# Moving the maxima's transfers to the front of a group's first slot, and splitting the shift around the small maximum

## The chip, the cores and the metric

The kernel runs on one NeuronCore of a Trainium2 chip. The metric is device time in microseconds of one execution, given as the median of several runs. The engines are named as the profile names them: PE is TensorE (PEld its weight loads), DVE is VectorE, ACT is ScalarE, POOL is GpSimd, and SP is SyncE, which issues most of the transfers.

## The reference

One transformer block over x of shape (4, 1024, 512) in float32, conditioned on a vector of 128 values per batch entry, with a further residual around the whole block:

```python
def _tc_rmsnorm(x, t, gw, gb, bw, bb):
    g = (t @ gw.T + gb)[:, None, :]
    b = (t @ bw.T + bb)[:, None, :]
    inv_rms = jax.lax.rsqrt(jnp.mean(x * x, axis=-1, keepdims=True) + EPS)
    return g * x * inv_rms + b

def _attention(x, Wq, Wk, Wv, Wo):            # 16 heads of 32
    q, k, v = ((x @ W.T).reshape(B, L, H, dh) for W in (Wq, Wk, Wv))
    p = jax.nn.softmax(jnp.einsum('blhd,bmhd->bhlm', q, k) / scale, axis=-1)
    return jnp.einsum('bhlm,bmhd->blhd', p, v).reshape(B, L, D) @ Wo.T

def _swiglu(x, gate_w, hid_w, out_w):         # hidden width 2048
    return jax.nn.silu(x @ gate_w.T) * (x @ hid_w.T) @ out_w.T

y = x + _attention(_tc_rmsnorm(x, t, g1w, g1b, b1w, b1b), Wq, Wk, Wv, Wo)
y = y + _swiglu(_tc_rmsnorm(y, t, g2w, g2b, b2w, b2b), gate_w, hid_w, out_w)
return x + y
```

## The kernel before

Tokens are handled in 8 blocks of 512 and heads in 4 groups of 4. Attention goes over 64 groups j: one block, one group of heads, and one half of the block's queries (256). A group has four slots (UN = 4), one for each 256 keys, and there are 256 slots r in all. A loop over g issues the work by hand, engine by engine, in program order; `kind = g % 4` is the slot's place in its group. What is done for one slot r is spread over later turns of the loop:

- `scores(r)` at g = r: sixteen TensorE matmuls into the PSUM tile `sc`. There is one such tile of four banks. `keep(r)` has ScalarE copy it to `raw[r]`, and `running_max` folds it into `rmax`.
- After the last slot of a group, at kind 0 of the next group, `max_blocks` transposes `rmax` in 32 by 32 blocks and reduces it on VectorE. `max_T` turns the small result with a matmul, reduces it once more on VectorE (`top`, 32 by 32) and sends it to DRAM (`tops`). `spread` reads it back as 1,024 values for all 128 partitions into the one buffer `shift`. So there are two transfers from SP, of which the second waits for the first to land.
- `shifted(r)` subtracts the maximum at g = r + 5, so that the last slot of a group is shifted at the next group's kind 0 and the next group's first slot at kind 1. `exponential(r)` follows in the same turn.
- `weighted(r)` at g = r + 6 multiplies with the values (`av`), and `accumulate(r)` has GpSimd issue a transfer that adds 1 MB of `raw` to the group's first slot, for the sums of the softmax. There are three of them per group, each waiting for the one before it.
- `take_sums` forms the sums of an earlier group with sixteen matmuls into the spare of the scores' PSUM tile (`spare`), and ScalarE copies them out (`total`). `max_T` uses the same spare tile and is issued after `take_sums`.

`spare` can only be written when `keep` has copied the scores, because it is the same PSUM memory.

What fills the rest of a turn depends on its time. Before g = 60 (about the first 650 us) `chain` issues one projection of keys, queries, values or outputs, and an even turn issues a second one, `late`. After that come the feed-forward products in pairs of turns: an even turn has `pair_26`, `copy_156` and the output products `one()` and `two()`; an odd turn has `pair_7`, `pair_3`, `pair_15`, and at its end `pair_4`, which waits for VectorE's `sub_5`.

TensorE, VectorE, ScalarE and GpSimd run their instructions in the order in which the loop issues them. SP's transfers are put in order by the framework's scheduler, which follows the order of issue and readiness; a transfer on SP that waits holds up those behind it. `pinned` holds the loads of keys, queries and values that belong to a turn.

In an even turn before the change, the order around the edit at kind 0 is, early: `max_blocks`, `shifted`, `late`, pinned loads, `weighted`, `keep`, `exponential`, `chain`, `take_sums`, `max_T`, `spread`, `running_max`. Late: the same up to `keep`, then `load_f`, `pair_26`, `copy_156`, `take_sums`, `max_T`, `exponential`, `one`, `two`, `running_max`, `spread`.

Of the kernel before, what the change touches and what calls it, by code (L numbers as in the profile page):

```python
# [12 lines left out]
ALU = mybir.AluOpType  # L13
# [10 lines left out]
def tile_cond_transformer_block(  # L24
# [13 lines left out]
    nc = tc.nc  # L38
# [8 lines left out]
    HG = P // DH  # L47
# [3 lines left out]
    UN = KT // 2  # L51
# [46 lines left out]
    raw, rmax, shift, av, acc, avs, oT = {}, {}, {}, {}, {}, {}, {}  # L98
# [230 lines left out]
    def spare(g: int):  # L329

        return ps_sc.tile([P, HG, 2, HQ], F32, tag="sc", name=f"spare{g}")

    def max_T(j: int, banks):
        pt = banks[:CHUNKS, 1, 0, :P]
        nc.tensor.matmul(pt, state.pop(("blocks", j)), ident, start=True, stop=True)
        top = sb.tile([CHUNKS, 32], F32, tag="top", name=f"top{j}")
        nc.vector.tensor_reduce(top, pt.rearrange("b (a q) -> b q a", a=P // 32), AX.X, ALU.max)
        state["top", j] = tc.dram_tile([CHUNKS, 32], F32, name=f"tops{j}")
        nc.sync.dma_start(out=state["top", j], in_=top)

    def spread(j: int):

        shift[j] = sb.tile([P, HG, HQ], F32, tag="shift", name=f"shift{j}")
        src = state.pop(("top", j)).rearrange("(o b) q -> o (b q)", o=1)
        nc.sync.dma_start(
            out=shift[j].rearrange("p h q -> p (h q)"), in_=src.to_broadcast([P, HG * HQ])
        )

    def shifted(r: int):
        s = shift[r // UN].unsqueeze(1).to_broadcast(list(raw[r].shape))  # L350
        nc.vector.tensor_tensor(raw[r], raw[r], s, ALU.subtract)  # L351

    def exponential(r: int):
        nc.scalar.activation(raw[r], raw[r], AF.Exp)  # L354
# [43 lines left out]
    def sums_out(j: int):  # L398
        state["total", j] = sb.tile([P, HQ], F32, tag="total", name=f"total{j}", bufs=2)
        nc.scalar.copy(state["total", j], state.pop(("sum", j)))  # L400
# [67 lines left out]
    def tokens(n: int):  # L468
        return [x2[n][:, k : k + 2, i * HQ : (i + 1) * HQ] for k in (0, 2) for i in range(2)]
# [23 lines left out]
    def product(dst, w, moving, start: bool = False):  # L493
        for k in range(2):
            mm(dst, w[:, k, :], moving[:, k, :], start and k == 0, k == 1, True)
# [17 lines left out]
    def pair_26(p: int):  # L513
        a = bank_a[p]
        product(a[:, LEFT], fw[p, 0][:, 1], tokens(p // NF)[2])
        product(a[:, RIGHT], fw[p, 1][:, 1], state["sums"][:, 1])

    def copy_156(p: int):
        if "b" not in state:

            state["b"] = ps_b.tile([P, NB], F32, tag="wb", name="pb")
            nc.tensor.matmul(state["b"], ones_mean, x2[0][:, 0, :], start=True, stop=True)
        bank_b[p] = state["b"]
        nc.scalar.copy(bank_b[p][:, RIGHT], bank_a[p][:, RIGHT])  # L524
# [46 lines left out]
    pinned = {}  # L571
# [36 lines left out]
    for b in range(1, B):  # L608
        for half in range(QB):
            s = math.ceil((len(queue) + 1) / PACE)  # L610
# [72 lines left out]
    with tc.manual_schedule(  # L683
# [37 lines left out]
        g = 0  # L721
# [22 lines left out]
        def take_sums(j: int, banks):  # L744

            if 0 <= j < NR // UN:
                sums(j, banks)
                sums_out(j)
                if j >= direct:
                    inverse(j)  # L750
                    normalize(j)

        while g < END:
            kind = g % UN
            r_x, r_v = g - UN - 1, g - UN - 2
            x_on, v_on = 0 <= r_x < NR, 0 <= r_v < NR
            j_m = g // UN - 1
            m_on = 0 <= j_m < NR // UN
            j_s = g // UN - 2
            s_on = 0 <= j_s < NR // UN  # L760
            j_n = g // UN - 3
            n_on = 0 <= j_n < NR // UN
            ffn = g >= FS
            p = (g - FS) // 2
            even = g % 2 == 0
            columns[0] = DH

            if g < NR:
                scores(g)
            if kind == 0 and m_on:  # L770
                max_blocks(j_m)
            if kind == 1 and j_n == GB + 1:
                normalize(GB)
            if x_on:
                shifted(r_x)
            if late is not None:
                late()
                late = None
            for fn, a in pinned.pop(g, []):
                fn(*a)  # L780
            if v_on:
                weighted(r_v)
                accumulate(r_v)
            if g < NR:
                keep(g)
            if kind == 1 and s_on:
                take_av(j_s)
            if kind == 0 and (m_on or n_on):
                banks = spare(g)
            due = bool(first) and first[0][0] <= g  # L790
            if not ffn:
                if x_on:
                    exponential(r_x)
                evict = chain(g, FG)
                if kind == 0 and n_on:
                    take_sums(j_n, banks)
                if kind == 0 and m_on:
                    max_T(j_m, banks)
                    spread(j_m)
                if g < NR:  # L800
                    running_max(g, 0)
                    running_max(g, 1)
                if evict is not None:
                    evict()
                for fn, a in halfway.pop(g, []):
                    fn(*a)
                if g == FS - 1:
                    columns[0] = DH
                    pair_15(0)
                    take_5(0)  # L810
                    add_15(0)
                elif even:
                    late = chain(g, FG)
                if g in (FS - 4, FS - 2):
                    load_f((g - FS + 4) // 2)
            elif even:
                load_f(p + 2)
                pair_26(p)
                copy_156(p)
                if kind == 0 and n_on:  # L820
                    take_sums(j_n, banks)
                if kind == 0 and m_on:
                    max_T(j_m, banks)
                if x_on:
                    exponential(r_x)
                one, two, evict = filler(p)
                one()
                two()
                if g < NR:
                    running_max(g, 0)  # L830
                    running_max(g, 1)
                if evict is not None:
                    evict()
                if kind == 0 and m_on:
                    spread(j_m)
                for fn, a in halfway.pop(g, []):
                    fn(*a)
            else:
                extra = due or len(queue) > FG
                evict = None  # L840
                if kind == 3 and extra:
                    evict = chain(g)
                pair_7(p)
                sub_5(p)
                pair_3(p)
                if kind == 3:
                    gate_tanh(p)
                if x_on:
                    exponential(r_x)
                pair_15(p + 1)  # L850
                take_5(p + 1)
                for fn, a in amid.pop(g, []):
                    fn(*a)
                if kind == 1:
                    gate_tanh(p)
                    if extra:
                        spare_bank[0] = True
                        evict = chain(g)
                if g < NR:
                    running_max(g, 0)  # L860
                if kind == 3 and evict is not None:
                    evict()
                if kind == 3:
                    gate(p)
                if g < NR:
                    running_max(g, 1)
                add_15(p + 1)
                if kind == 1:
                    gate(p)
                    if evict is not None:  # L870
                        evict()
                pair_4(p)
                hidden(p)
                if due:
                    chain(g)()
                for fn, a in halfway.pop(g, []):
                    fn(*a)
            if kind == 0 and n_on and j_n < direct:
                inverse(j_n)
                if j_n % GB == GB - 1:  # L880
                    normalize(j_n)
            if kind == 2 and n_on and j_n < direct and j_n % GB != GB - 1:

                if j_n != GB:
                    normalize(j_n)
            columns[0] = DH
            for fn, a in ended.pop(g, []):
                fn(*a)
            if g == FS + 2 * FG - 2:
                load_ow(0)  # L890
            g += 1
# [90 lines left out]
```

## Time and profile before

| | |
|---|---|
| median of 3 runs | 2914.73 us (2912.62 to 2918.55) |
| profiled execution | 2911.5 us, span 2909.7 us |
| PE busy | 2449.3 us (84%) |
| DVE busy | 1908.1 us (66%) |
| ACT busy | 1330.1 us (46%) |
| mean granted TensorE clock | 0.924 |
| accumulates (POOL queue) | 192 of 1 MB, 9.3 us to landing (median) |
| broadcasts of the maxima (SP queue) | 64 of 512 KB, 5.1 us to landing (median) |

A line of the profile's groups gives source line, engine, operation, output and inputs, shapes and count; then busy time and mean duration; then how long the engine stood idle just before these instructions and what released it. Names such as `raw` or `pb` are the kernel's tiles with numbers left out. Line 93 is the helper through which most matmuls go, so that its groups are told apart by their tiles. `SPq` and `POOLq` lines are instructions that issue a transfer. In a timeline, the bracket at the end of a line holds the idle time before it and its releaser.

### The profile page before, as it was taken

The page shows a single profiled execution, that of the slowest core. Times are in us where ns is not written, and L with a number is a line of the kernel's source. Part 1 is how long each engine was busy: PE and PEld are TensorE (multiplying, and loading weights), DVE is VectorE, ACT ScalarE, POOL GpSimd, SP SyncE. Part 2 cuts the span into 40 slices and gives each one's busy share as a digit, 9 for nine tenths or more (in the row PEclk, how much of TensorE's full clock was granted, in tenths as well). Part 3 has the DMA queues.
Part 4 walks back from the last instruction along what each step waited for, and adds up shares of the span by engine and source line. Part 5 has one row for each costly group of instructions (what it writes and reads, how often), then busy time and mean ns, then how long its engine had stood idle before and what let it go on. Part 6 is the DMA issues. An engine that isn't in the chain of part 4 may idle for free. (4 is left out here: it accounts for less than half of the span.)

```text
span 2909.7 us, 71319 instructions
## 1 busy us (share of the span) xinstructions
PE 2449.3 (84%) x31866; PEld 1157.2 (40%) x31866; DVE 1908.1 (66%) x2048; ACT 1330.1 (46%) x1303; POOL 172.4 (6%) x205
## 2 busy tenths in 40 slices
PE   8778778888788888887988878887888788889999
PEld 3233223334344443443444434444344344444444
DVE  2667666757667776776677757776678667863332
ACT  4555555555345544554455435544455445532111
POOL 0000000000000000000000000000000000000000
PEclk9899889999899989998999989999999899999999
DMA  5697788877777777777767767777677777773442
GB/s 197 195 242 205 204 218 202 209 176 187 184 187 192 194 188 171 192 185 203 183 178 186 194 174 192 190 196 182 167 197 197 187 184 173 183 206 111 138 134 81
DMA packets 198270, 535.53 MB, mean 184 GB/s; under 512 B 25415, under 2 KB 82759, under 8 KB 170574
## 3 DMA queue, kind: packets, MB, share of 16 engines
q0 software_dynamic: 28656, 208.68, 37.2%
q1 hardware_dynamic: 169022, 322.29, 33.5%
q8 instruction: 251, 4.11, 0.6%
q14 instruction: 53, 0.43, 0.0%
q10 hardware_dynamic: 288, 0.01, 0.0%
HBM read 279.99 MB, written 42.23 MB: 111 GB/s over the span
## 5 line engine op out<-in xcount | busy, mean ns | idle before, releaser
L351 DVE TENSOR_TENSOR raw<-raw,shift 128x2048 f32<-128x2048 f32 x256 | 584.9, 2285 | 418.4 <-DMA shift<-tops 418.4
L354 ACT ACTIVATE raw<-raw 128x2048 f32<-128x2048 f32 x256 | 489.4, 1912 | 600.4 <-DVE raw L351 599.6
L304 ACT COPY raw<-sc 128x2048 f32<-128x2048 f32 x256 | 477.8, 1867 | 364.5 <-PE sc L297 233.4
L309 DVE TENSOR_TENSOR rmax<-rmax,raw 128x1024 f32<-128x1024 f32 x384 | 468.7, 1221 | 40.8 <-ACT raw L304 34.7
L93 PE MATMUL pc<-h,ow 128*32 128x512 f32 x4096 | 477.1, 594 | 0.5 <-DMA ow<-in_out_w 0.5
L93 PE MATMUL pb<-sums,fa 128*32 128x256 f32 x2048 | 170.0, 459 | 271.4 <-DVE pb L531 271.4
L364 PE MATMUL av<-raw,v 128*32 128x256 f32 x4096 | 304.6, 420 | 101.6 <-ACT raw L354 101.4
L297 PE MATMUL sc<-q,k 32*128 32x256 f32 x4096 | 330.5, 442 | 0.1
L378 POOL DMA_DIRECT2D raw<-raw x192 | 165.7, 863 | 2412.1 <-ACT raw L354 1472.1
L297 PEld LDWEIGHTS sc<-q,k 32*128 32x128 f32 x4096 | 206.1, 206 | 205.6 <-issue 127.1
L93 PE MATMUL pa<-x,fa 128*32 128x256 f32 x4096 | 270.0, 381 | 9.9 <-issue 9.2
L93 PE MATMUL pa<-sums,fw 128*32 128x256 f32 x4096 | 268.2, 379 | 0.4 <-issue 0.4
L93 PE MATMUL pkq<-y,wkq 128*32 128x512 f32 (+1 forms) x1976 | 248.0, 623 | 4.1 <-ACT y L183 4.1
L93 PEld LDWEIGHTS pc<-h,ow 128*32 128x32 f32 x4096 | 165.3, 110 | 208.7 <-issue 137.5
L562 DVE SCALAR_TENSOR_TENSOR res<-pc,res 128x512 f32<-128x512 f32 x128 | 88.5, 692 | 196.5 <-PE pc L93 196.5
L364 PEld LDWEIGHTS av<-raw,v 128*32 128x32 f32 x4096 | 113.9, 117 | 255.3 <-ACT raw L354 110.4
L93 PEld LDWEIGHTS pb<-sums,fa 128*32 128x32 f32 x2048 | 69.0, 124 | 346.4 <-DVE pb L531 300.7
L93 PEld LDWEIGHTS pa<-x,fa 128*32 128x32 f32 x4096 | 134.1, 112 | 118.2 <-issue 30.2
L93 PEld LDWEIGHTS pa<-sums,fw 128*32 128x32 f32 x4096 | 132.9, 110 | 89.0 <-issue 0.9
L541 ACT ACTIVATE t<-pa 128x512 f32<-128x512 f32 x128 | 76.7, 599 | 153.6 <-PE pa L93 153.6
L93 PE MATMUL po<-oT,wo 128*32 128x512 f32 x1024 | 127.8, 643 | 14.8 <-DVE h L546 11.7
L524 ACT COPY pb<-pa 128x256 f32<-128x256 f32 x128 | 45.7, 357 | 203.1 <-PE pa L93 182.5
(92 smaller groups left out, 2017.3 us busy)
## 6 DMA issues: line engine op xcount, KB each, us to landing
raw<-raw POOLq DMA_DIRECT2D x192, 1024.0 KB, 9.3
fw<-sw SPq DMA_DIRECT2D x128, 512.0 KB, 7.4
fa<-in_gh_w SPq DMA_DIRECT2D x128, 384.0 KB, 4.3
shift<-tops SPq DMA_DIRECT2D x64, 512.0 KB, 5.1
ow<-in_out_w SPq DMA_DIRECT2D x128, 256.0 KB, 6.2
wkq<-in_kq_w SPq DMA_DIRECT2D x32, 512.0 KB, 6.4
v<-vs SPq DMA_DIRECT2D x128, 128.0 KB, 5.9
k<-kqs SPq DMA_DIRECT2D x124, 128.0 KB, 7.3
```

Of the source, the lines that this page charges most:

```text
L93: nc.tensor.matmul(dst[k : k + n, :], w[:, k : k + n], moving, start=start, stop=stop, skip_group_check=seeded)
L297: nc.tensor.matmul(sc[:, i, k, :], keys[rows, k * P : (k + 1) * P], queries[rows, :], start=True, stop=True)
L304: nc.scalar.copy(raw[r].rearrange("p k h q -> p h k q"), state.pop(("sc", r)))
L309: nc.vector.tensor_tensor(rmax[j], rmax[j], raw[r][:, k, :, :], ALU.max)
L351: nc.vector.tensor_tensor(raw[r], raw[r], s, ALU.subtract)
L354: nc.scalar.activation(raw[r], raw[r], AF.Exp)
L364: nc.tensor.matmul(av[j][i * DH : (i + 1) * DH, :], v[m, u][:, k, i * DH : (i + 1) * DH], raw[r][:, k, i, :], start=(kt == 0), stop=(kt == ...
L378: nc.gpsimd.dma_start(out=acc[j].rearrange("p k h q -> p (k h q)"), in_=raw[r].rearrange("p k h q -> p (k h q)"), accum_op=ALU.add,)
L524: nc.scalar.copy(bank_b[p][:, RIGHT], bank_a[p][:, RIGHT])
L541: nc.scalar.activation(state["t", p], bank_a[p], AF.Tanh, scale=0.5)
L562: nc.vector.scalar_tensor_tensor(r, pp, 0.5, r, ALU.mult, ALU.add)
```

## The change

At kind 0 alone, the shift of the previous group's last slot is cut in two halves of two heads each. The small maximum's matmul, reduction and both transfers are issued between them. `take_sums`, `max_T` and `spread` move ahead of the projection in the early turns, ahead of `load_f` in the late ones, and ahead of the pinned loads in both. The exponential and the pinned loads follow the second half. In late turns `pair_26` and `copy_156` are issued first, as they were, and `load_f` after them. Turns of kind 1 to 3 keep their order.

```diff
-    def shifted(r: int):
-        s = shift[r // UN].unsqueeze(1).to_broadcast(list(raw[r].shape))
-        nc.vector.tensor_tensor(raw[r], raw[r], s, ALU.subtract)
+    def shifted(r: int, heads: slice = slice(0, HG)):
+        t = raw[r][:, :, heads, :]
+        s = shift[r // UN][:, heads, :]
+        nc.vector.tensor_tensor(t, t, s.unsqueeze(1).to_broadcast(list(t.shape)), ALU.subtract)
...
-            if x_on:
+            if x_on and kind:
                 shifted(r_x)
...
-            for fn, a in pinned.pop(g, []):
-                fn(*a)
+            if kind:
+                for fn, a in pinned.pop(g, []):
+                    fn(*a)
...
-            if kind == 0 and (m_on or n_on):
-                banks = spare(g)
+            if kind == 0 and ffn:
+                pair_26(p)
+                copy_156(p)
+            if kind == 0:
+                if m_on or n_on:
+                    banks = spare(g)
+                if n_on:
+                    take_sums(j_n, banks)
+                if x_on:
+                    shifted(r_x, slice(0, HG // 2))
+                if m_on:
+                    max_T(j_m, banks)
+                    spread(j_m)
+                if x_on:
+                    shifted(r_x, slice(HG // 2, HG))
+                for fn, a in pinned.pop(g, []):
+                    fn(*a)
...
                 evict = chain(g, FG)
-                if kind == 0 and n_on:
-                    take_sums(j_n, banks)
-                if kind == 0 and m_on:
-                    max_T(j_m, banks)
-                    spread(j_m)
...
                 load_f(p + 2)
-                pair_26(p)
-                copy_156(p)
-                if kind == 0 and n_on:
-                    take_sums(j_n, banks)
-                if kind == 0 and m_on:
-                    max_T(j_m, banks)
+                if kind:
+                    pair_26(p)
+                    copy_156(p)
...
-                if kind == 0 and m_on:
-                    spread(j_m)
```

## The prediction

> **What bounds the kernel now.** I read the page first, then the waits split at 650 us (before it TensorE projects keys, queries and values between attention slots; after it the feed-forward products are interleaved), then the timeline of one group of four slots in each part. Part five of the page (line, engine, operation, tiles, count, then busy us, mean ns, then idle before it and its releaser):
>
> ```profile
> L351 DVE TENSOR_TENSOR raw<-raw,shift 128x2048 f32<-128x2048 f32 x256 | 584.9, 2285 | 418.4 <-DMA shift<-tops 418.4
> L93 PE MATMUL pb<-sums,fa 128*32 128x256 f32 x2048 | 170.0, 459 | 271.4 <-DVE pb L531 271.4
> L364 PE MATMUL av<-raw,v 128*32 128x256 f32 x4096 | 304.6, 420 | 101.6 <-ACT raw L354 101.4
> ```
>
> TensorE is busy 2449.3 of 2909.7 us; of its 460 us idle, 271 and 101 end on VectorE's sub_5 and on the exponential. Both are queued behind the first shift of a group, which waits for the broadcast of the maxima: 418.4 us over 64 groups. The waits by part say where (us, times, longest). 20 to 650 us:
>
> ```profile
> DVE raw L351 <- DMA shift<-tops: 118.4, 14, 14.9
> PE av L364 <- ACT raw L354: 101.4, 15, 11.1
> DVE top L337 <- PE spare L335: 37.6, 14, 3.4
> PE spare L335 <- ACT total L400: 18.9, 12, 3.4
> ```
>
> 650 to 2600 us:
>
> ```profile
> DVE raw L351 <- DMA shift<-tops: 300.0, 50, 15.3
> PE pb L93 <- DVE pb L531: 271.4, 49, 14.9
> ```
>
> Only in the early part does VectorE wait for TensorE before it can form the small maximum: 14 times, 2.7 us each. Timeline of an early group (start, duration):
>
> ```profile
> 450.93 1.85 ACT L304 COPY raw<-sc 128x2048 f32<-128x2048 f32 x1
> 453.03 2.28 DVE L351 TENSOR_TENSOR raw<-raw,shift 128x2048 f32<-128x2048 f32 x1
> 457.16 0.35 ACT L400 COPY total<-spare 128x256 f32<-128x256 f32 x1
> 458.01 0.28 DVE L337 TENSOR_REDUCE top<-spare 32x32 f32<-32x128 f32 x1 [2.70 <-PE spare L335]
> 458.31 0.32 SPq L339 DMA_DIRECT2D tops<-top  x1
> 459.99 0.86 POOL L378 DMA_DIRECT2D raw<-raw  x1 [10.58 <-DMA raw<-raw]
> 461.75 0.32 SPq L345 DMA_DIRECT2D shift<-tops  x1
> 471.24 2.29 DVE L351 TENSOR_TENSOR raw<-raw,shift 128x2048 f32<-128x2048 f32 x1 [9.70 <-DMA shift<-tops]
> 475.53 1.93 PE L364 MATMUL av<-raw,v 128*32 128x256 f32 x16 [5.84 <-ACT raw L354]
> ```
>
> The maximum goes out at 458.31, is back for the broadcast at 461.75, and the broadcast lands 9.5 us later, behind the 1 MB accumulate issued at 459.99. A late group:
>
> ```profile
> 1518.32 2.28 DVE L351 TENSOR_TENSOR raw<-raw,shift 128x2048 f32<-128x2048 f32 x1
> 1520.52 0.27 DVE L337 TENSOR_REDUCE top<-spare 32x32 f32<-32x128 f32 x1
> 1520.82 0.32 SPq L339 DMA_DIRECT2D tops<-top  x1
> 1526.80 0.32 SPq L345 DMA_DIRECT2D shift<-tops  x1
> 1527.43 0.86 POOL L378 DMA_DIRECT2D raw<-raw  x1 [10.42 <-DMA raw<-raw]
> 1531.88 2.29 DVE L351 TENSOR_TENSOR raw<-raw,shift 128x2048 f32<-128x2048 f32 x1 [5.91 <-DMA shift<-tops]
> ```
>
> Here max_T's matmuls are done (1520.10) before the shift ends; the accumulate of 1516.14 is in flight, and the maximum lands (1526.80) just as that accumulate does (its successor starts at 1527.43). The broadcast then precedes the next accumulate and takes 5.1 us.
>
> **What the skill says.** "TensorE: Matmul & The Clock Gate", Part 1: after an idle window of about 3.4 us the array runs at half clock until it has been busy for one. The trace agrees: after the 5.51 us stall that ends at 1534.57, the window below has a granted clock of 0.56 (last columns: clock, DMA share, GB/s). "DMA: Bandwidth & Descriptors", "Anatomy of one DMA": about 2 us of fixed cost; the smallest tops transfer here takes 2.9 us from issue to the next step. The same page, "Queues, rings and completion order": the queues share 16 engines and alternate packet by packet. The trace agrees only in part, since the 4 KB of maxima come out as late as the whole accumulate. "VectorE: DVE Perf Modes", "The TRN2 errata": f32 tensor_tensor costs (N+151)/0.96 ns; 2285 and 1221 ns for 2048 and 1024 elements agree.
>
> ```profile
> 1534.00:1541.00 7.00, 6.43 (x64) 3.10 (x68) 6.86 (x9) 4.54 (x4) 0.00 (x0) 0.56 0.85 248
> ```
>
> **The change, early part (14 groups).** In slot 0 TensorE now runs sums and max_T before the projection, ScalarE copies the totals before the exponential, and SP issues tops and broadcast before the projection's store and the next weight or gate load (one to three issues).
>
> (1) Time of the small maximum. From late groups, sums to max_T takes 1.95 us; sums start when keep ends. In the group shown keep ends at 452.78, so the maximum comes at about 454.9, not 458.0: 3.1 us earlier. Over the groups, keep's end lies 3.85 to 6.9 us before the maximum: 1.8 to 4.8 us, mean 2.7. The totals' copy no longer stands behind an exponential.
>
> (2) Landing of tops, now 5.2 us after issue on average (2.9 to 8.1). It cannot land before the accumulate in flight does; that keeps about half the groups from the full gain, while those held by a store or load just ahead (one by a 1 MB y load) gain more. The broadcast's issue moves 2.9 us earlier on average.
>
> (3) Landing of the broadcast, now 7.6 us mean, 8.7 to 9.5 where an accumulate was issued first. The last accumulate of a group waits for the exponential of slot 0, and that moves behind the small maximum: 0.27 + 1.22 (second half of the shift) + 1.9 us, so it ends 3.4 us after the maximum starts; tops needs 0.3 + 2.9 = 3.2. So the broadcast goes out first, as late groups do, and I take 5.2 us: 2.4 us less.
>
> (4) Together 5.3 us. The fourteen stalls of TensorE at av were 5.2, 10.6, 11.1, 4.7, 8.4, 7.9, 9.9, 7.9, 10.2, 5.8, 6.2, 2.5, 7.1 and 3.1 (sum 100.7); less 5.3 each, not below zero, leaves 32. Gain 69 us. If the landing doesn't improve, 2.9 us gain 40; if every stall vanishes, 100.
>
> (5) Half clock after these stalls costs 1.75 us each now (av 1.93 for 1.07, the next product about 0.9 more): 24 us. Seven stalls over 2.5 us remain, at 1.2: gain 16 (10 to 24).
>
> (6) Cost: TensorE waits for keep's copy before sums (about 1.6 us) and for the totals' copy (0.75), where the projection covered the first: 13 x 2.35 = 30 us against 18.9 now, so 11, and 4 more of half clock (0 to 16). Behind these waits stand the projection and the next scores; nothing else hides them.
>
> (7) SP: broadcast and what follows wait for tops' landing as before; the store and loads put behind it are needed two products (over 7 us) later. The single shift buffer also makes the broadcast wait for the second half, done 1.4 us after the maximum starts, inside tops' 2.9.
>
> **The change, late part (50 groups).** In the built program the order on TensorE and ScalarE, and of tops and broadcast on SP, is as before; only the shift is split around the maximum. A half costs 1.22 us, so 0.16 more per pair, 10 us of VectorE in all, hidden by its 300 us of waiting. The maximum starts when max_T is done: 0.42 to 1.06 us earlier, mean 0.57 (nothing in each eighth group, where SP is held by a load). But tops still lands with the accumulate in flight, so I take 3 us in all; the ends are -5 and 28, with less half clock 41. The exponential starts up to 0.94 us later; next slot's av leaves 1.7 to 2.0 us, and 0.94 only where the delay is 0.35. Without that cover it would cost 45. In the first late group the last accumulate (now 1.4 us ahead of the broadcast) falls behind it: 3.4 us.
>
> Sum: 69 + 16 - 11 - 4 + 3 + 3 = 76 us. The profiled execution took 2911.5 (span 2909.7, 1.8 around it): 2835.5. The median shown, 2914.7, is 3.2 above it: 2838 (2912.62 to 2918.55 spread alone is 0.2%, about what a measurement can tell from no change).
>
> **Rivals.** (A) The late part gains too, if tops' landing follows its issue and not the accumulate: 41 in place of 3, 2800. For it: in a few late groups tops lands 3.1 us after issue, near its floor. Against: in nearly all it lands 0.2 us after the accumulate. (B) The early broadcast stays behind the accumulate: 40 + 8 - 15 + 3 = 36 gained, 2878. For it: broadcast and accumulate are both released by one landing, tenths of a us apart; against: the exponential's new place. (C) Slower: TensorE's wait between av and sums in slot 0. If accumulates and not issue decide the broadcast's landing, nothing comes back, and 13 x (1.9 + 0.8) = 35 us against 19, plus 16 of half clock, cost 32: 2947. It decides once the broadcast lands less than about 2 us earlier. Against: ten of the 13 early tops transfers that have an accumulate in flight land over 1.5 us after it, so issue and what is queued just ahead count. (D) Nothing measurable, gain and cost in balance.
>
> **Numbers.** Forecast 0.60 (own range 2808 to 2864), A 0.14, B 0.16, D 0.03, C 0.07. The range 2785 to 2888 takes in A and B and leaves out the rest. Faster by over 0.2%: 0.90; within 0.2%: 0.03; slower: 0.07.
>
> **What would show it.** Right: up to 650 us, VectorE's wait for shift falls from 118 to about 45 and TensorE's at av from 101 to about 32; the wait of top for TensorE is small; a wait of spare for the copy of the scores appears, 1.6 us each; late, the pb stall stays between 255 and 275. Wrong: the broadcast in early groups still lands over 7 us after issue, or the pb stall falls by 25 or more, or the late av begins to wait for the exponential.

## The result and the profile after

| | before (run beside it) | after |
|---|---|---|
| median | 2916.64 us (2912.62 to 2920.25, 4 runs) | 2889.14 us (2887.16 to 2894.1, 4 runs) |
| profiled execution, span | 2911.5, 2909.7 us | 2888.1, 2886.3 us |
| first feed-forward turn (scores at g = 60) starts at | 651.3 us | 623.9 us |
| from there to the last scores | 1909.2 us | 1911.4 us |
| rest | 349.2 us | 351.0 us |

The ratio of after to before is 0.9909 (95% interval 0.9889 to 0.9928). The kernel became faster by about 27 us where 76 were forecast, and the time lies 1 us above the range. The third to fifth rows of the table, read from the start of the first scores' matmuls, say where: the early part gave 27.4 us, and the late part and the rest took 4 back. So of the prediction's cases it is rival B, the early broadcast that stays behind the accumulate.

The page of after, part five. The shift counts 320 instructions now, since 64 of the 256 are cut in two:

```profile
L352 DVE TENSOR_TENSOR raw<-raw,shift 128x2048 f32<-128x2048 f32 (+1 forms) x320 | 593.6, 1855 | 400.3 <-DMA shift<-tops 400.3
L93 PE MATMUL pb<-sums,fa 128*32 128x256 f32 x2048 | 170.0, 459 | 272.5 <-DVE pb L532 272.4
L365 PE MATMUL av<-raw,v 128*32 128x256 f32 x4096 | 300.8, 415 | 62.0 <-ACT raw L355 61.9
L93 PE MATMUL pkq<-y,wkq 128*32 128x512 f32 (+1 forms) x1976 | 249.0, 629 | 10.1 <-DMA wkq<-in_kq_w 6.0
```

The late stall at pb stayed (271.4 before). The one at av fell from 101.4 to 61.9, and a wait of 6.0 us for a projection's weights is new. The waits between 20 and 640 us (us, times, longest):

```profile
DVE raw L352 <- DMA shift<-tops: 104.6, 14, 11.8
PE av L365 <- ACT raw L355: 58.0, 13, 9.0
DVE top L337 <- PE spare L335: 20.1, 13, 2.7
PE spare L394 <- ACT raw L304: 19.6, 12, 2.7
```

VectorE's wait for `shift` was to fall from 118 to about 45 us and fell to 104.6. TensorE's wait at av was to fall to 32 and is 58.0. The wait of the sums for `keep`'s copy is there as expected, 1.6 us each. Between 640 and 2600 us:

```profile
DVE raw L352 <- DMA shift<-tops: 299.1, 50, 15.8
PE pb L93 <- DVE pb L532: 272.4, 47, 15.4
```

Nothing moved here. The timeline of an early group shows the step that failed:

```profile
426.82 1.85 ACT L304 COPY raw<-sc 128x2048 f32<-128x2048 f32 x1
428.73 1.07 PE L394 MATMUL spare<-raw,ones_sum 128*32 128x256 f32 x16 [1.80 <-ACT raw L304]
430.73 0.28 DVE L337 TENSOR_REDUCE top<-spare 32x32 f32<-32x128 f32 x1 [0.58 <-PE spare L335]
431.04 0.32 SPq L339 DMA_DIRECT2D tops<-top  x1
432.17 1.91 ACT L355 ACTIVATE raw<-raw 128x2048 f32<-128x2048 f32 x1 [1.94 <-DVE raw L352]
436.33 0.86 POOL L379 DMA_DIRECT2D raw<-raw  x1 [11.02 <-DMA raw<-raw]
437.20 0.32 SPq L345 DMA_DIRECT2D shift<-tops  x1
447.22 2.29 DVE L352 TENSOR_TENSOR raw<-raw,shift 128x2048 f32<-128x2048 f32 x1 [11.82 <-DMA shift<-tops]
451.51 1.08 PE L365 MATMUL av<-raw,v 128*32 128x256 f32 x8 [7.36 <-ACT raw L355]
```

`keep` ends at 428.67 and the maximum starts 2.1 us later; in the group shown of before it was 5.2 us. The exponential of the group's last slot ends at 434.08, but the last accumulate doesn't wait for it at all: it starts at 436.33, 0.5 us after the accumulate before it has landed. The maxima come back 0.9 us after that, at 437.20, and the broadcast lands 10.0 us later, behind the accumulate.

Thirteen early groups have accumulates in flight. In eight of them it goes as in this one: the maxima come back 1.4 to 5.2 us after the second accumulate has landed, and 0.9 to 3.6 us after the last one has started. In the other five they are back within 0.4 us of that landing or before it, and the broadcast goes out first. The last accumulate starts 0.5 us after the landing in 11 groups, and 0.3 us after the exponential's end in two.

Added up in the early part: TensorE waits 43.4 us less at av, 10.7 more for `spare` (the copies of scores and totals) and 6.0 more for weights, which is 26.7 of the 27.4 us gained. Its busy time fell by 0.7 us.

### The profile page after: what moved, and what is told of

Its sections match the earlier page's. It is cut to its first block, busy times and chain, and to the rows that moved or that the text cites. A ratio compares the mean times of both kernels' runs of the same rounds, so it can differ in the third digit from the quotient of the medians.

```text
span 2886.3 us, 71384 instructions
## 1 busy us (share of the span) xinstructions
PE 2450.7 (85%) x31866; PEld 1168.4 (40%) x31866; DVE 1915.6 (66%) x2112; ACT 1332.1 (46%) x1303; POOL 172.0 (6%) x205
## 5 line engine op out<-in xcount | busy, mean ns | idle before, releaser
L352 DVE TENSOR_TENSOR raw<-raw,shift 128x2048 f32<-128x2048 f32 (+1 forms) x320 | 593.6, 1855 | 400.3 <-DMA shift<-tops 400.3
L365 PE MATMUL av<-raw,v 128*32 128x256 f32 x4096 | 300.8, 415 | 62.0 <-ACT raw L355 61.9
L93 PEld LDWEIGHTS pkq<-y,wkq 128*32 128x32 f32 (+1 forms) x1976 | 93.0, 117 | 139.1 <-issue 90.2
```

The costliest lines, as they stand in the source:

```text
L93: nc.tensor.matmul(dst[k : k + n, :], w[:, k : k + n], moving, start=start, stop=stop, skip_group_check=seeded)
L352: nc.vector.tensor_tensor(t, t, s.unsqueeze(1).to_broadcast(list(t.shape)), ALU.subtract)
L365: nc.tensor.matmul(av[j][i * DH : (i + 1) * DH, :], v[m, u][:, k, i * DH : (i + 1) * DH], raw[r][:, k, i, :], start=(kt == 0), stop=(kt == ...
```

## The experiments

Two questions stood after this. Early: is it the last accumulate ahead of the broadcast that keeps the gain away (the theory), or the other transfers around it, which the change has moved too, or the late landing of the maxima (the rivals)? Late: what would have to be changed for the stall at pb to fall? All runs are compared with the kernel before, run beside them. Columns three to eight are added up by group from each trace (the pb column counts every stall there, whatever ended it, and so lies some 1.2 us above the lines of the waits): early means the groups before the first feed-forward turn; "tops" is from the issue of the maxima's transfer to the broadcast's issue, "broadcast" from its issue to the shift that waits for it, both mean us of a group.

| run | median us, ratio (95%) | first f.-f. turn | early broadcast | early av stall | late pb stall | late tops | late broadcast |
|---|---|---|---|---|---|---|---|
| before | 2914.73 | 651.3 | 7.62 | 101.4 | 272.6 | 5.19 | 5.57 |
| after | 2889.14, 0.9909 (0.9889 to 0.9928) | 623.9 | 7.00 | 58.0 | 273.7 | 5.77 | 5.53 |
| e1 | 2856.94, 0.9804 (0.9768 to 0.9839) | 588.3 | 4.34 | 30.4 | 268.0 | 5.72 | 5.49 |
| e2 | 2760.77, 0.9478 (0.9438 to 0.9518) | 625.9 | 6.72 | 58.6 | 159.6 | 4.66 | 4.33 |
| e3 | 2887.57, 0.9928 (0.9889 to 0.9967) | 620.6 | 6.72 | 54.2 | 275.6 | 5.29 | 5.50 |
| e4 | 2830.97, 0.9724 (0.9692 to 0.9756) | 592.2 | 5.38 | 31.0 | 250.4 | 5.46 | 5.84 |
| e5 | 2690.22, 0.9207 (0.9172 to 0.9242) | 577.6 | 4.89 | 26.0 | 148.6 | 4.47 | 4.72 |
| e6 | 2701.76, 0.9251 (0.9223 to 0.928) | 588.4 | 4.62 | 22.0 | 144.1 | 4.49 | 4.58 |
| e7 | 2881.62, 0.9842 (0.9791 to 0.9893) | 610.4 | 4.77 | 63.6 | 284.4 | 5.43 | 5.53 |
| e8 | 2839.36, 0.9709 (0.9671 to 0.9747) | 635.7 | 7.37 | 64.5 | 224.5 | 5.84 | 4.52 |
| e9 | 2916.66, 0.9997 (0.9977 to 1.0017) | 650.8 | 7.41 | 97.6 | 275.6 | 5.97 | 5.40 |
| e10 | 2708.49, 0.93 (0.9273 to 0.9327) | 590.8 | 4.72 | 48.5 | 139.7 | 3.92 | 4.56 |

### e1: the last accumulate held behind the broadcast, early only

GpSimd issues the accumulates in program order, so a copy of one value of `shift` ahead of the group's last accumulate keeps that accumulate back until the broadcast has landed.

```diff
+    def after_broadcast(j: int):
+        tick = sb.tile([1, 1], F32, tag="tick", name=f"tick{j}")
+        nc.gpsimd.tensor_copy(tick, shift[j][0:1, 0, 0:1])
...
                 weighted(r_v)
+                if kind == 1 and g < FS and g // UN - 1 in shift:
+                    after_broadcast(g // UN - 1)
                 accumulate(r_v)
```

> The changed kernel, with one edit: before 650 us the last accumulate of a group is held until the broadcast of the maxima has landed (GpSimd first reads one value of shift). Theory (the broadcast is slow because the last accumulate is issued some tenths of a us before it): all early broadcasts land 4.5 to 5.5 us after issue (now 3.7 to 10.0), TensorE's stall at av before 640 us falls from 58 to about 25 us, and the time is 30 to 50 us below the changed kernel's 2889, near 2850. Rival (loads and stores in SP's own queue make it slow): landings as now, 2883 to 2900.

Measured: 2856.94 us, and the early part ends 36 us sooner than in after. The waits between 20 and 620 us:

```profile
DVE raw L352 <- DMA shift<-tops: 80.8, 15, 8.2
PE av L365 <- ACT raw L355: 30.4, 13, 6.5
```

And the timeline of the group shown of after:

```profile
412.62 0.32 SPq L339 DMA_DIRECT2D tops<-top  x1
418.12 0.32 SPq L345 DMA_DIRECT2D shift<-tops  x1
422.73 2.29 DVE L352 TENSOR_TENSOR raw<-raw,shift 128x2048 f32<-128x2048 f32 x1 [5.75 <-DMA shift<-tops]
422.76 2.30 POOL L387 COPY tick<-shift 1x1 f32<-1x1 f32 x1 [13.00 <-DMA shift<-tops]
```

The maxima are still 5.5 us on their way, but the broadcast now lands in 4.6 us (10.0 in after). Every early broadcast takes 3.6 to 4.8 us, and av's stall is 30.4 us. The maxima take longer in this run than in after (6.8 for 5.8 us over the early groups), and the stall still falls by 27.6 us, so the slow broadcast is the accumulate's doing. That the maxima come back too late to be first is a question of its own, and e4 bears on it. The edit moves none of the projection's transfers, the other rival; e7 tests that one on the kernel before.

### e3: the shift of slot 0 whole

Is the small maximum's place between two halves worth anything by itself?

```diff
                 if x_on:
-                    shifted(r_x, slice(0, HG // 2))
+                    shifted(r_x)
                 if m_on:
                     max_T(j_m, banks)
                     spread(j_m)
-                if x_on:
-                    shifted(r_x, slice(HG // 2, HG))
```

> The changed kernel with the shift of slot 0 undivided again, ahead of the small maximum; everything else stays moved. Theory (the whole gain lies in the order before 650 us, and the split buys nothing, since the maxima land with the accumulate): 2889 within 6 us, pb stall 265 to 280. Rival (the earlier small maximum is worth its half us in each group): pb stall 290 or more and 2905 to 2925.

Measured: 2887.57 us, 1.6 below after with intervals that cover each other (0.9889 to 0.9967 against 0.9889 to 0.9928). The split is worth nothing that was measured; the gain comes from what stays moved, above all `take_sums`, `max_T` and `spread` ahead of the projection.

### e4: the maxima sent from ScalarE's queue

```diff
-        nc.sync.dma_start(out=state["top", j], in_=top)
+        nc.scalar.dma_start(out=state["top", j], in_=top)
```

> The changed kernel with the small transfer of the maxima to DRAM issued from ScalarE's queue; the broadcast stays on SP. Theory (accumulates in flight hold the maxima in the late part; SP's loads and stores only in the early part): late landings as now, pb stall 260 to 280; early maxima land up to 2.5 us sooner, the broadcast gets ahead of the last accumulate in some more groups, 2865 to 2889. Rival (SP's own queue holds them throughout): late maxima land 3 us after issue, pb stall under 180, under 2800.

Measured: 2830.97 us, below the 2865 to 2889 of the theory and above the rival's 2800. The waits of TensorE at av (20 to 620 us) and at pb (620 to 2600 us), one line from each answer:

```profile
PE av L365 <- ACT raw L355: 31.0, 13, 6.0
...
PE pb L93 <- DVE pb L532: 247.6, 48, 11.3
```

From issue to the broadcast's issue the maxima take about what they took: 5.62 us early (5.83 in after), 5.46 late (5.77). What decides the order, though, is when they are back as against the landing of the second accumulate, and that has changed: in 10 of 13 early groups they are back within 0.3 us of it or before it (five in after, within 0.4). Group 8, counted from 0, first in after and then here:

```profile
387.70 0.32 SPq L339 DMA_DIRECT2D tops<-top  x1
394.34 0.86 POOL L379 DMA_DIRECT2D raw<-raw  x1 [11.72 <-DMA raw<-raw]
395.40 0.33 SPq L345 DMA_DIRECT2D shift<-tops  x1
...
376.86 0.31 ACTq L339 DMA_DIRECT2D tops<-top  x1
382.56 0.32 SPq L345 DMA_DIRECT2D shift<-tops  x1
382.96 0.86 POOL L379 DMA_DIRECT2D raw<-raw  x1 [11.82 <-DMA raw<-raw]
```

The maxima left 6.1 us before the landing in after and 5.6 us before it here; they were back 1.6 us after it there and 0.1 us after it here. Groups 6, 8 and 12 are late by 1.5 to 2.9 us in each of the five traces of the changed kernel in which SP sends the maxima (after, e1, e2, e3, e8), and by at most 0.3 us here. So in most early groups it is SP's own queue that brings them back too late to be first; which of the transfers in it does so is not shown, and groups 7, 10 and 11 stay late by 2.0 to 5.3 us for a reason that is open.

The broadcast is ahead of the accumulate in the 10 groups, and takes 4.1 to 5.1 us there, 8.1, 9.2 and 8.1 in the other three. The early part of the theory was right, then, and its effect was underrated: the early part ends at 592.2 us, about where e1's does, with no accumulate held. Late, the gain of 23 us at pb was in neither expectation: in every eighth group SP is held by a load when the maximum is ready (the transfer leaves some 4 us after the maximum starts), and it no longer stands behind that load (the longest of pb's waits falls from 15.4 to 11.3 us).

### e2: two accumulates held, late only

In after, the broadcast is already ahead of the last accumulate in 38 of the 50 late groups. What the maxima run against there is the second accumulate, in flight when they are sent. Here it waits with the third.

```diff
                 weighted(r_v)
-                accumulate(r_v)
+                if not ffn or kind not in (0, 1):
+                    accumulate(r_v)
+                elif kind == 0:
+                    held = r_v
+                else:
+                    if g // UN - 1 in shift:
+                        after_broadcast(g // UN - 1)
+                    accumulate(held)
+                    accumulate(r_v)
```

> The changed kernel, with one edit: from the first feed-forward turn on, the second and third accumulates of a group are both held until the broadcast of the maxima has landed. Theory (in the late part the maxima land with the accumulate in flight, not by their own issue): tops lands 3 to 4 us after issue instead of 5.5, the broadcast 5 us later, TensorE's stall at pb falls from 272 to 150 us or less, with less half clock after it, and the time is 2700 to 2800. Rival (the loads ahead in SP's queue hold the maxima): tops still takes over 5 us, the stall stays near 270, the delayed accumulates cost something, 2885 to 2930.

Measured: 2760.77 us. The waits between 640 and 2600 us:

```profile
DVE raw L352 <- DMA shift<-tops: 178.9, 49, 10.4
...
PE pb L93 <- DVE pb L536: 158.4, 44, 10.0
```

The stretch from the first feed-forward turn to the last scores shrinks from 1911 to 1768 us. In that stretch TensorE idles 100 us less (314.7 to 214.6: 112 at pb, with 13 given back at `spare`), and its busy time falls from 1596.7 to 1553.8 us for the same products, while its mean granted clock rises from 0.92 to 0.95. The maxima take 4.66 us late, 1.1 less than in after and not the 3 to 4 that were expected, with no accumulate in the way:

```profile
1246.30 0.32 SPq L339 DMA_DIRECT2D tops<-top  x1
1251.58 0.33 SPq L345 DMA_DIRECT2D shift<-tops  x1
1256.32 2.29 DVE L352 TENSOR_TENSOR raw<-raw,shift 128x2048 f32<-128x2048 f32 x1 [4.50 <-DMA shift<-tops]
1258.60 0.55 POOL L379 DMA_DIRECT2D raw<-raw  x1
```

So an accumulate in flight is only a part of what delays the maxima late. What the rest is stays open; a load of 384 KB for the feed-forward products that SP issues some 6 us ahead is a suspect, and was not tried.

### e8: only the last accumulate held, late

Does e2's gain come from the second accumulate or the third?

```diff
                 weighted(r_v)
+                if kind == 1 and ffn and g // UN - 1 in shift:
+                    after_broadcast(g // UN - 1)
                 accumulate(r_v)
```

> The changed kernel with only the last accumulate held until the broadcast has landed, in the late part. Theory (in the late part it is the second accumulate, in flight when the maxima leave, that holds them; the last one follows the broadcast anyway): landings as in the changed kernel, pb stall 260 to 280, 2880 to 2895. Rival (the last accumulate is what slows the late broadcast, and the run that held two gained by that): pb stall below 200, under 2800.

Measured: 2839.36 us, where the theory had no change (2880 to 2895) and the rival under 2800. The waits between 640 and 2600 us:

```profile
DVE raw L352 <- DMA shift<-tops: 249.3, 50, 11.0
...
PE pb L93 <- DVE pb L536: 223.3, 48, 10.6
```

The maxima take what they took (5.84 us), but the broadcast lands in 4.52 instead of 5.53 us. Two kinds of groups are mixed in this. In the 38 late groups of after in which the broadcast was issued first, by 0.1 to 1.1 us, it now takes 4.57 us instead of 5.20 (5.13 in e1, which leaves the late part as it is), so an accumulate that follows closely cost it 0.6 us; these groups bring 15 of the 49 us at pb. In the other 12 the last accumulate was issued 1.8 to 11.9 us ahead of the broadcast in after, and the broadcast falls from 6.59 (6.65 in e1) to 4.35 us; they bring 34. The theory had overlooked that these 12 are not in the order of the rest. TensorE's busy time in the late stretch falls by another 10 us (1596.7 to 1586.7). Of e2's 114 us at pb, some 49 are the third accumulate's and the rest come with the second.

The early part of this run, whose code is after's, ends at 635.7 us, against 623.9 in after and 625.9 in e2, with the accumulate first in 10 of 13 groups instead of eight: so much is the race worth from one execution to the next. The late stretch varies as well where nothing in it is changed (before 1909.2, e7 1923.9; after 1911.4, e1 1900.8), so single executions tell no early or late differences below some 15 us.

### e7: the hold of e1 on the kernel before

```diff
                 weighted(r_v)
+                if kind == 1 and g < FS and g // UN - 1 in shift:
+                    after_broadcast(g // UN - 1)
                 accumulate(r_v)
```

> The kernel before, with only the hold of the last accumulate until the broadcast has landed, before 650 us. Theory (the order of broadcast and last accumulate is a cost of its own, which the change did not remove): early broadcasts land in about 5 us instead of 7.6, TensorE's stall at av falls from 101 by about 30, and the time is 25 to 45 us below the kernel before. Rival (the hold helps only where the maxima leave early): within 10 us of the kernel before.

Measured: 2881.62 us, 33 less than before. Here nothing is moved but the accumulate, and the early broadcast goes from 7.62 to 4.77 us. The transfers of the projections that the change moved lie as in before, so they are not what made the early broadcast slow. Nor is the change needed for this gain; e1 has 22 us more in the early part (588.3 against 610.4), which is what the change brings with it; that it is the earlier maximum is likely and was not tested apart.

### e9: the late half of the change alone

The early turns keep before's order; late turns have after's.

```diff
-            if x_on and kind:
+            if x_on and (kind or not ffn):
                 shifted(r_x)
...
-            if kind == 0:
+            if kind == 0 and ffn:
                 if m_on or n_on:
                     banks = spare(g)
...
                 evict = chain(g, FG)
+                if kind == 0 and n_on:
+                    take_sums(j_n, banks)
+                if kind == 0 and m_on:
+                    max_T(j_m, banks)
+                    spread(j_m)
```

> The changed kernel with the order of the kernel before restored in the early turns, so that only the late turns are changed. Theory (all that the change brings lies before 650 us, the late part brings nothing): the time of the kernel before, 2905 to 2925, first feed-forward turn at about 651 us, pb stall 265 to 285. Rival (the late half of the change carries part of the gain): 2900 or less.

Measured: 2916.66 us in 14 runs against 2911.47 in 19, ratio 0.9997 (0.9977 to 1.0017). No difference: the 50 late groups bring nothing, and cost nothing.

### e5, e6 and e10: the edits together

e5 has e4's queue, e1's hold in all groups and e2's second hold in the late ones. e6 holds the second accumulate in the early groups too: `ffn` falls out of both conditions. e10 puts e5's three edits into the kernel before.

```diff
                 weighted(r_v)
-                accumulate(r_v)
+                if kind == 0 and ffn:
+                    held = r_v
+                else:
+                    if kind == 1 and g // UN - 1 in shift:
+                        after_broadcast(g // UN - 1)
+                    if kind == 1 and ffn:
+                        accumulate(held)
+                    accumulate(r_v)
```

> The changed kernel with three edits together: the last accumulate of a group held behind the broadcast before 650 us, the last two held after it, and the small transfer of the maxima on ScalarE's queue. Theory (accumulates in flight and SP's loads hold the maxima one behind the other, so the gains add): early as with the early hold or better (first feed-forward turn by about 585 us), late maxima land 3.5 us after issue (4.8 with the hold alone), pb stall near 110, 2670 to 2725. Rival (the edits save the same time): 2755 within 15.

> As the one with three edits, but the last two accumulates are held in the early part as well. Theory: the early maxima no longer land with the second accumulate, so that they land about 3 us after issue, the early av stall falls below 20 us, and it is 10 to 25 us faster than with the last alone held early. Rival (the accumulates fall behind and come to hold the sums): slower by 10 or more.

> The kernel before with the three edits of the fastest version (last accumulate held early, last two held late, small transfer on ScalarE's queue), and without the change. Theory (the change's own worth is an earlier small maximum in the early part, here not limited by the last accumulate any more): the first feed-forward turn comes 15 to 30 us later than with the change (577.6), the late part the same within 10; 2700 to 2725. Rival (with the accumulates held, the change is worth nothing): 2685 to 2700.

Measured: e5 takes 2690.22 us, the fastest kernel here: 199 us below after. Its page, part two (40 slices: busy tenths of TensorE, and the clock granted to it), and its waits between 640 and 2600 us:

```profile
PE   8888889898988989888989888898988898889999
PEclk9999999998999999999999999999999999999999
```

```profile
DVE raw L352 <- DMA shift<-tops: 165.0, 46, 7.2
...
PE pb L93 <- DVE pb L536: 143.1, 44, 6.6
```

TensorE is busy 89% of the span (85% in after) and the mean clock is 0.959 (0.927). The stall at pb missed its 110, because the late maxima again take 4.47 us.

e6 is 11.5 us slower than e5 (2701.76 against 2690.22; the intervals of the ratios, 0.9172 to 0.9242 and 0.9223 to 0.928, overlap a little, the four runs of each do not), and its early part ends 10.8 us later. The maxima gain 1.2 us there and av 4, but the waits for `spare` grow from 33.7 to 42.7 us. Behind them stands a wait that e5 doesn't have (20 to 620 us):

```profile
ACT raw L304 <- DMA raw<-raw: 11.1, 7, 4.1
```

In seven groups `keep`'s copy in slot 0 starts only when an accumulate of an earlier group has landed (once one lands at 183.22 and the copy starts at 183.32), and the sums wait for `keep`. So the accumulates that were held twice land too late, as the expectation's rival had it, though they hold `keep`'s copy first.

e10 says what the change is still worth once the accumulates are held. Its median lies 18 us above e5's, with intervals that don't overlap (0.9273 to 0.9327 against 0.9172 to 0.9242). In the profiled executions its early part is 13 us longer and its late part 11 shorter (1753 against 1764). Both are within what single executions vary by, so the change remains a gain of 18 us by the medians and of about 27 us by the ratios, but its place is not shown.

## Why the prediction was wrong, by its steps

**Step (1), the small maximum 2.7 us earlier: right.** From `keep`'s end to the maximum it was 4.77 us and is 2.25, mean of the 12 early groups that form sums: 2.5.

**Step (2), the broadcast's issue 2.9 us earlier: too large.** The maxima took 5.17 us from their issue to the broadcast's and now take 5.83. From `keep`'s end to the broadcast's issue it was 10.04 us over the 14 early groups and is 8.43, so 1.6 us arrived. The step had a reason for a shortfall, the accumulate in flight, and took it as a bound ("cannot land before"), which it isn't: the maxima came back 2.4 us ahead of that landing in one group of before and 1.2 us ahead in one of after. In the groups that lost most they come back well after the landing, and e4 puts most of that down to SP's own queue, in which the step saw only what would no longer be in the way.

**Step (3), "So the broadcast goes out first, as late groups do, and I take 5.2 us": this step failed.** It let the last accumulate wait for the exponential of slot 0, 3.4 us after the maximum starts, and let the maxima come back after 0.3 + 2.9 = 3.2 us. Neither held. The last accumulate's second release is the landing of the one before it (the POOL line at 459.99 in the prediction's early timeline showed it: released by a DMA of raw, not by the exponential). In the group shown of after the exponential ended 2.25 us before the accumulate started, and it was the later of the two releases in 2 groups of 13. And the maxima came back after 5.83 us, not 2.9, which was the smallest value of before, where 5.2 was the mean. Even in the two groups where the exponential did hold the accumulate, they came 2.7 and 1.9 us after it.

The prediction's own rival C had the count that speaks against this step: in ten of 13 early groups the maxima came back over 1.5 us after the accumulate in flight, while the next one starts 0.5 us after that landing. So the order is not a matter of tenths either, as rival B had it. In the 8 early groups of after in which the accumulate is still first, by 0.9 to 3.6 us, the broadcast takes 6.9, 9.2, 8.7, 9.3, 10.0, 7.8, 9.1 and 8.2 us; in four of the other five it takes 4.5, 4.6, 4.5 and 4.3 (in the fifth no shift waits for it). In before the accumulate was issued first in all 13, and not only where the broadcast took 8.7 us or more, as the step read it: 5.9 to 10.0 us in 11 of them, 4.0 and 4.8 in two. The mean fell from 7.6 to 7.0, not to 5.2. e1 shows that the accumulate ahead is the cause: with it behind, 4.34, which is even less than step (3) had hoped; and e4 shows that what makes the maxima late is for the most part SP's queue.

**Step (4), together 5.3 us per group and 69 us at av: failed with (3).** 1.6 us and 0.6 make 2.2 us a group, and the stall at av fell by 43.4, or 3.1 a group. The rest fits the waits of step (6): TensorE, held 0.8 us a group longer for `spare`, comes to av that much later itself. The sum took the two as independent. In e1 30.4 us of stall remain where 32 was forecast, but that is in part luck: there the broadcast lands 4.1 us earlier after `keep`, not 5.3, and the waits for `spare` are 14.5 us longer than in before.

**Step (5), 16 us of half clock back: missed.** TensorE's busy time in the early part, 509.5 us from 20 us on, is 508.8 in after. The stalls that remain are still long enough, up to 9 us, and the new waits bring half clock of their own: in five of the early groups a stretch of 3.4 us at a clock of 0.5 begins during or within 2.3 us after the waits of sums and maximum. Stretches of one such group of after, whose sums waited 1.84 us until 266.04 (last columns: clock, DMA share, GB/s):

```profile
264.00:267.20 3.20, 1.27 (x20) 0.42 (x16) 2.04 (x3) 2.01 (x3) 0.86 (x1) 0.99 1.11 370
267.20:270.40 3.20, 2.80 (x17) 1.51 (x21) 2.12 (x3) 1.03 (x2) 0.00 (x0) 0.50 1.08 233
270.60:273.00 2.40, 2.40 (x28) 1.29 (x24) 2.37 (x4) 1.07 (x2) 0.00 (x0) 1.00 0.49 97
```

TensorE was busy 1.27 of the 3.2 us ahead of the slow stretch, in which the projection begins. The Trainium skill ("TensorE: Matmul & The Clock Gate", Part 1) has half clock follow an idle window of about 3.4 us; no single wait here was that long, but a stretch with TensorE busy for two fifths of it was enough. The term was also too large: in e1, with the stalls that step (4) forecast, busy time is 502.8, so 6.7 us came back.

**Step (6), 11 us more for the copies: right**, 10.7 (29.6 for 18.9). The 4 us of half clock beside it can't be told apart from (5).

**Step (7), loads behind the broadcast needed more than 7 us later: missed in one group.** One projection waits 6.00 us for its weights, in the timeline of after:

```profile
135.82 1.93 PE L93 MATMUL pkq<-y,wkq 128*32 128x512 f32 x8 [6.00 <-DMA wkq<-in_kq_w]
```

The load was issued at 121.50, 0.1 us ahead of the last accumulate. With that accumulate held this wait is gone (0.1 us in e1, none in e5), and in e2, e3, e4 and e8, which don't hold it early, it is 5.1 to 5.6 us. In e7 there is none either (before's order). I had priced the delay of the issue, and not the accumulate that the load then meets.

**The late part, 3 us: right in substance.** It gained nothing (1909.2 to 1911.4 us; e9 at 0.9997). The first late group's stall did fall by the 3.4 us of the prediction, and later groups gave them back. "As late groups do" held for 36 of the 50 late groups of before and for 38 of after, in which the broadcast goes first. One of them:

```profile
1493.45 0.32 SPq L339 DMA_DIRECT2D tops<-top  x1
1499.95 0.32 SPq L345 DMA_DIRECT2D shift<-tops  x1
1500.08 0.86 POOL L379 DMA_DIRECT2D raw<-raw  x1 [10.10 <-ACT avs L387]
1505.32 2.29 DVE L352 TENSOR_TENSOR raw<-raw,shift 128x2048 f32<-128x2048 f32 x1 [6.34 <-DMA shift<-tops]
```

**The rivals.** B was priced at 36 us and 2878; 27.5 were measured. It took 2.9 us for step (2) where 1.6 came, and had no 6 us for the weights. A is refuted by e9. C's waits came to 10.7 us more, where it had 16, and it needed a broadcast that lands less than 2 us earlier; it landed 2.2 us earlier, close to that point.

**The sum again, with what was measured:** 43.4 at av, less 10.7 for `spare`, less 6.0 for weights, 0.7 of clock, and 4.0 lost in the late part and the rest (within what executions vary by): 23.4 us, which is the difference of the spans. Of the 27.5 us between the medians 4 are not in these two profiled executions.

## What to carry to other kernels

Before work is pulled forward to send a small transfer sooner, see what it comes back with and what stands ahead of it in its own queue: if it comes back after a large one has landed, and the next large one is let go by that landing, an earlier issue is worth little, and holding the large one back is worth much (here 32 us early and 128 late, against 27 for the change); a queue with nothing ahead was worth 58. Never set the best value of one wait against the mean of another in a race of two transfers; take both from the same groups. And a transfer that sits off the critical path, as the accumulates do, still deserves a look when it shares the engines with one that sits on it.

## What the runs showed of the hardware

- Two large transfers on different queues, issued close together, are not served alike. In the early groups of after the 512 KB broadcast takes 4.3 to 4.6 us when it is ahead of the 1 MB accumulate (by 0.2 to 1.7 us) and 6.9 to 10.0 when it is behind it (by 0.9 to 3.6); the accumulate takes 10.8 to 13.3 us behind the broadcast and 8.3 to 10.5 ahead of it. In the late groups the broadcast's means are 5.20 (38 groups ahead) and 6.59 us (12 behind). The Trainium skill ("DMA: Bandwidth & Descriptors", Queues, rings and completion order) has each engine take turns between queues packet by packet; the 0.6 us that a following accumulate costs the broadcast (e8) fits that, the advantage of being first is larger than I had read from it.
- 4 KB of maxima take 5 to 6 us on the mean from issue to the next step with an accumulate in flight (after, e4), and 4.7 and 4.5 in late groups with both held (e2, e5). The smallest seen is 1.34 us, in the first group of after, which has no accumulate in flight. The fixed cost of about 2 us that the prediction quotes is its section's figure for transfers that GpSimd issues; the maxima leave from SP.
- A queue of its own leaves that mean within 0.3 us (e4), but lets the maxima come back with the landing of the accumulate in flight in 10 of 13 early groups instead of five.
- The copy of one value on GpSimd took 2.30 us in e1 and e2, and started and ended with VectorE's subtraction of 2.29 us. The Trainium skill ("SBUF — State Buffer", SBUF: two separate sides) says that a VectorE instruction with two inputs in SBUF and a GpSimd one that reads SBUF exclude each other on a shared port; the lines shown agree with that. In one of e2's 50 groups the copy started first, 0.04 us ahead of the subtraction, and took 0.18 us. The held accumulates thus start some 2 us after the broadcast has landed, and not with it.
